# Weights requested behind the products that free their buffer, and small products of 48 keys in banks held for a stage

## The chip, the cores and the metric

The kernel runs on one core of a Trainium2 chip. The core has five engines with a queue each: TensorE (PE; its weight loads are shown apart, as PEld), VectorE (DVE), ScalarE (ACT), GpSimd (POOL) and SyncE (SP), which here issues all DMA transfers. The metric is the device time of one execution in microseconds, lower is better. Everything is in float32.

## The reference

The input x has 48 x 48 tokens of 768 channels. Layer 0 is a transformer block with 12 heads of 64 channels; layer 1 is a Fourier mixing layer, which the change doesn't touch. Cut to what matters here:

```
xn = layernorm(x, ln1_g, ln1_b)
q, k, v = split_heads(xn @ qkv_w + qkv_b)                # 12 heads, 2304 tokens, 64
attn = (q * scale) @ k.T                                   # 2304 x 2304 for each head
rel_h[h, w, kh] = q[h, w] . rel_pos_h[h - kh + 47]       # 48 numbers for each query
rel_w[h, w, kw] = q[h, w] . rel_pos_w[w - kw + 47]       # 48 numbers for each query
attn[(h, w), (kh, kw)] += rel_h[h, w, kh] + rel_w[h, w, kw]
out = softmax(attn) @ v
x = x + out @ proj_w + proj_b ; x = x + mlp(layernorm(x)) ; then layer 1
```

The "small products" of the title are `rel_h` and `rel_w`: for one row (or column) of queries, 48 queries against 48 rows of a table of 64 channels.

## The kernel before

Heads are worked on in six pairs, one head on partitions 0 to 63 and one on 64 to 127. The stage of projections lasts until about 453 us of the profile, the attention until about 1525 us, and then come the output projection, the MLP and layer 1.

**Projections** (`queries_keys_values`). Three passes p = 0, 1, 2 take 768 tokens each. At the start of a pass, `channels_first` transposes two groups of normalised rows into `xt`, and `sums_of_tokens` adds parts of them. Nine blocks follow: six calls of `queries_and_keys`, one for each head pair, and three of `values`. The order is written by hand in `orders`: in pass 0 the pairs come first, in pass 1 the values come first, and in pass 2 it is pair 0, the three values, and pairs 1 to 5. Each block forms a 2 x 2 product in seven products instead of eight (`seven`), of three matmul instructions each, and each instruction is recorded as two matmuls. The seven products rotate over four banks, `m0` to `m3`; evictions are L395 and L426 on ACT and L397, L399 and L428 on DVE. The four results of a block go through output tiles `o` (pool `stage`, 7 buffers) and are stored by SP (L429 for queries and keys, L460 for values).

The weights of a pair lie in one of two buffers, `pairs[slot]`. `weights_of` issues two DMAs of 384 KB each on SP (L348) and then four additions on POOL (`left`, L152 to L155), which form the sums that the seven products need; the value weights are fetched by `weights_of_values` (L334, two DMAs) and have additions of the same kind, three times as long. Where weights are asked for is written in the loop:

```
now = ahead
if pairs_left:
    ahead = weights_of(pairs_left.pop(0), slot % 2)
    slot += 1
queries_and_keys(p, i, *now)
```

Behind a block other work may be attached: `arrive` fetches three row tiles of x (L364 on SP) and normalises them (`normalise`, L116 to L124, mostly on DVE), after blocks 1 and 2 of the passes 0 and 1; `weights_of_values` after blocks 3 and 4 of pass 0; `constants` after block 5 of it; in pass 2, `fetch`, `columns` (twice after each of blocks 1 to 3), `relative` (after blocks 4, 6 and 8) and `fetch_values` (after block 5), which prepare pair 0 for the attention.

**Small products.** `columns(pr, i)` makes `rel_w` for 8 columns of queries, and `relative(pr, c)` makes `rel_h` for 8 rows. Each is 8 x 2 matmul instructions (L251, tile `wp`; L273, tile `hp`): one for each head of the pair, on array columns 0 to 63 and 64 to 127, with 48 queries moving and 64 rows of the table `relT` as weights, of which the kernel later uses 48. The queries of `columns` lie 16 elements apart in SBUF, those of `relative` in runs of 16. `two_parts` then splits the bank in a high and a low part (L222, L223 on ACT, L224 on DVE). `relative` also issues 24 DMAs on SP (L286, L290) that spread these parts into the tile `terms`.

The bank of a small product is a new tile for each call:

```
def small_bank(name):
    return banks["small"].tile([P, G], F32, name=name, tag="small")
```

In the stage of projections its pool has two buffers, in the attention one, which it shares with `den`, the sums of the softmax (L555).

**Attention.** For a pair and a group of 384 queries, `scores` (L525, L531, L535) runs over 18 tiles of 128 keys, in two runs of nine; `products` (L540) multiply the exponentials of the run before by v; `columns` and `relative` of what comes next, and `finish` of the last group, stand between the parts of `products`.

The order on PE and SP is that of the program (`manual_schedule`). The order on DVE, ACT and POOL is worked out by a scheduler when the program is built, so an edit on SP can move instructions there.

Of the kernel before, what the change touches and what calls it, by code (L numbers as in the profile page):

```python
# [9 lines left out]
F32 = mybir.dt.float32  # L10
# [5 lines left out]
PSUM = bass.MemoryType.PSUM  # L16
DRAM = bass.MemoryType.DRAM

P = 128
HW = 48  # L20
# [9 lines left out]
G = 384  # L30
# [14 lines left out]
def block_then_afno(  # L45
# [25 lines left out]
    nc = tc.nc  # L71
# [113 lines left out]
    with ExitStack() as flag_scope:  # L185
# [11 lines left out]
        with ExitStack() as att:  # L197
# [4 lines left out]
            relT = cst.tile([P, 2, 2, 112], F32, name="relT")  # L202
# [2 lines left out]
            r_pool = att.enter_context(tc.tile_pool(name="att_r", bufs=2))  # L205
            b_pool = att.enter_context(tc.tile_pool(name="att_b", bufs=3))

            banks = {}

            def small_bank(name):  # L210
                return banks["small"].tile([P, G], F32, name=name, tag="small")

            copies = [0]

# [29 lines left out]
            def columns(pr, i):  # L244

                qT = heads[pr][0].rearrange("p (c b h w) -> p b w c h", c=6, b=3, h=8)
                ps = small_bank("wp").rearrange("p (w c h) -> p w c h", w=8, h=8)
                for r in range(8):
                    w = 8 * i + r
                    for j in range(2):  # L250
                        nc.tensor.matmul(  # L251
                            ps[ts(j, 64), r], relT[:, j, 1, 47 - w : 111 - w],
                            qT[:, w // 16, w % 16], start=True, stop=True,
                        )
                hi, lo = (
                    a.rearrange("p (c b h w) -> p b w c h", c=6, b=3, h=8)[
                        :, i // 2, ds(8 * (i % 2), 8)
                    ]
                    for a in (col_hi, col_lo)
                )  # L260
                two_parts(hi, lo, ps)
# [3 lines left out]
            def relative(pr, c):  # L265

                qT = heads[pr][0][:, ts(c, G)].rearrange("p (b h w) -> p h b w", b=3, h=8)
                hp = small_bank("hp")
                ps = hp.rearrange("p (b h w) -> p h b w", b=3, h=8)
                for r in range(8):  # L270
                    h = 8 * c + r
                    for j in range(2):
                        nc.tensor.matmul(  # L273
                            ps[ts(j, 64), r], relT[:, j, 0, 47 - h : 111 - h], qT[:, r],
                            start=True, stop=True,
                        )
                row_hi = r_pool.tile([P, G], F32R, name="row_hi")
                row_lo = r_pool.tile([P, G], F32R, name="row_lo")
                two_parts(row_hi, row_lo, hp)
                terms = b_pool.tile([P, 3, 3, G], F32R, name="terms")  # L280
                ready[pr, c] = terms
                for j in range(2):
                    for n, (row, column) in enumerate(((row_hi, col_hi), (row_lo, col_lo))):
                        for i in range(3):
                            rows = ds(64 * j + 16 * i, 16)
                            nc.sync.dma_start(  # L286
                                out=terms[ds(64 * j + 16 * n, 16), i].bitcast(F32),
                                in_=row[rows].bitcast(F32).unsqueeze(1).to_broadcast([16, 3, G]),
                            )
                            nc.sync.dma_start(  # L290
                                out=terms[ds(64 * j + 32 + 16 * n, 16), :, i].bitcast(F32),
                                in_=column[rows, ts(c, G)].bitcast(F32)
                                .unsqueeze(1).to_broadcast([16, 3, G]),
                            )
# [11 lines left out]
            def queries_keys_values(qkv):  # L306
# [18 lines left out]
                upool = qkv.enter_context(tc.tile_pool(name="qkv_u", bufs=2))  # L325
                ln1 = qkv.enter_context(tc.tile_pool(name="ln1", bufs=3))
                psum = qkv.enter_context(tc.tile_pool(name="ps_qkv", bufs=1, space=PSUM))
                banks["small"] = qkv.enter_context(tc.tile_pool(name="ps_q", bufs=2, space=PSUM))

                wv = wpool.tile([P, NC, C], F32, name="wv")  # L330
                wvs = wpool.tile([P, 3, 3, CH], F32, name="wvs")
# [13 lines left out]
                def weights_of(pr, slot):  # L345
                    w, ws = pairs[slot]
                    for i in range(2):
                        nc.sync.dma_start(  # L348
                            out=w[:, :, i],
                            in_=qkv_w[:, ds(i * C + pr * P, P)].rearrange("(c p) f -> p c f", p=P),  # L350
                        )
                    left(
                        nc.gpsimd, w[:, 0:3, 0], w[:, 3:6, 0], w[:, 0:3, 1], w[:, 3:6, 1],
                        [ws[:, i] for i in range(3)],
                    )
                    return w, ws
# [114 lines left out]
                    orders.append(work)  # L471

                pairs_left = [i for work in orders for kind, i in work if kind == 0]
                ahead = weights_of(pairs_left.pop(0), 0)
                slot = 1
                for p in range(T // TB):
                    for g in (2 * p, 2 * p + 1):
                        channels_first(g)
                    sums_of_tokens(xt, xs)
                    for n, (kind, i) in enumerate(orders[p]):  # L480
                        if kind:
                            values(p, i)
                        else:
                            now = ahead
                            if pairs_left:
                                ahead = weights_of(pairs_left.pop(0), slot % 2)
                                slot += 1
                            queries_and_keys(p, i, *now)

                        if p == 0 and n in (3, 4):  # L490
                            weights_of_values(n - 3)
                        elif (p, n) == (0, 5):
                            constants()
                        elif p < 2 and n in (1, 2):
                            arrive(2 * p + 1 + n)
                        if p == 2 and n == 0:
                            fetch(0)
                        elif p == 2 and n in (1, 2, 3):
                            for j in (0, 1):
                                columns(0, 2 * (n - 1) + j)  # L500
                        elif p == 2 and n in (4, 6, 8):
                            relative(0, n // 2 - 2)
                        elif p == 2 and n == 5:
                            fetch_values(0)

            with tc.manual_schedule(engines={mybir.EngineType.PE, mybir.EngineType.SP}):
# [1 line left out]
                    queries_keys_values(qkv)  # L508

                psum = att.enter_context(tc.tile_pool(name="ps_att", bufs=1, space=PSUM))  # L510
                banks["small"] = psum
                kv_b = att.enter_context(tc.tile_pool(name="att_kv_b", bufs=1))
                o_pool = att.enter_context(tc.tile_pool(name="att_o", bufs=2))
                kv = [None, kv_b]
# [35 lines left out]

                def finish(pr, c, acc, ot):

                    den = small_bank("den")
                    for j in range(2):
                        nc.tensor.matmul(  # L555
                            den[ts(j, 64)], ones[:, 0:64], acc[:, j, :], start=True, stop=True
                        )
                    at = pr * (T // G) + c
                    rden = o_pool.tile([P, G], F32, name="rden", bufs=1)
                    nc.scalar.activation(  # L560
                        rden, den, AF.Identity, accum_out=sums[:, at : at + 1]
                    )

                    nc.vector.scalar_tensor_tensor(
                        ot, rden, col(V_VB + pr), ot, ALU.mult, ALU.add
                    )
                    nc.vector.reciprocal(rden, rden)  # L567
                    o = o_pool.tile([P, G], F32, name="o")
                    nc.vector.tensor_tensor(by_rows(o), by_blocks(ot), by_blocks(rden), ALU.mult)
                    nc.gpsimd.tensor_tensor(inverse, inverse, rden, ALU.add)  # L570
                    nc.sync.dma_start(out=oT[ts(pr, P), ts(c, G)], in_=o)
# [5 lines left out]
                for n, (pr, c, u) in enumerate(runs):  # L577
# [9 lines left out]
                    for i in range(RUN):  # L587
                        kt = RUN * u + i
                        p = exps[:, (RUN * n + i) % 18]
# [4 lines left out]
                    small = []  # L594
                    if u and c < 3:
                        small.append(partial(relative, pr, c + 3))
                    if pr < NC - 1:
                        if (c, u) in ((3, 1), (4, 0), (4, 1)):
                            i = 2 * (2 * (c - 3) + u - 1)
# [55 lines left out]
        with tc.tile_pool(name="ps_flag", bufs=1, space=PSUM) as psum, tc.tile_pool(  # L655
            name="ps_early", bufs=2, space=PSUM
# [29 lines left out]
        with tc.If(safe < 1):  # L686
            with ExitStack() as att:
                xnT = main.rearrange("p (c t) -> p c t", c=NC)
                with tc.tile_pool(name="g_ln1", bufs=3) as ln1, tc.tile_pool(
                    name="g_ps_ln1", bufs=2, space=PSUM  # L690
# [8 lines left out]
                psum = att.enter_context(tc.tile_pool(name="ps_gen", bufs=2, space=PSUM))  # L699
# [6 lines left out]
                relT = cst.tile([HD, 2, 112], F32, name="g_relT")  # L706
# [8 lines left out]
                for pr in range(NC):  # L715
                    w3 = []
                    for n, name in enumerate(("g_wq", "g_wk", "g_wv")):
                        w = w_pool.tile([P, NC, P], F32, name=name)
# [36 lines left out]
                    for sg in range(T // SG):  # L755
# [20 lines left out]
                        for i in range(2):  # L776
                            hp = psum.tile([P, G], F32, name="g_hp", tag="m")
                            for r in range(8):
                                h = sg * 16 + i * 8 + r
# [13 lines left out]
                        for i in range(2):  # L793
                            wp = psum.tile([P, 24, 16], F32, name="g_wp", tag="m")
                            for r in range(24):
                                w = i * 24 + r
# [584 lines left out]
```

## Time and profile before

| | us |
|---|---|
| median of 3 runs (3062.34 to 3068.3) | 3062.45 |
| the profiled execution | 3062.51 |
| its span, from the first to the last instruction | 3060.7 |
| PE busy | 2963.6 |
| DVE busy | 1783.4 |
| ACT busy | 868.6 |
| POOL busy | 572.1 |
| POOL waiting for `in_qkv_w_dram` in L152 | 345.5 |
| PE matmuls of L417 (`queries_and_keys`), 756 records | 253.0 |
| `wp` (L251), 1152 records, busy | 56.1 |
| `hp` (L273), 1152 records, busy | 40.7 |

Busy time of an engine is the time in which at least one of its instructions ran; PE and PEld overlap. A row of the groups names line, engine, operation, what is written and read, shapes and count, then busy time and mean duration in ns of one, then the idle time of the engine just ahead of it and what ended that. In a timeline the first column is the start, the second the length in us of a merged stretch, and "x32" the number of instructions in it. Rows of matmuls give the active rows and columns of the array ("128*64") and the moving shape ("128x48").

### The profile page before, as it was taken

The numbers are of one execution on the slowest core, as the hardware profiler recorded it, in microseconds if no ns is written. First come the engines' busy times: TensorE is split into PE (matmuls) and PEld (weight loads), VectorE is DVE, ScalarE is ACT, GpSimd is POOL, SyncE is SP. The second block draws the span as 40 slices with busy tenths as digits, with TensorE's granted clock in tenths as the row PEclk, the third lists the DMA queues.
The fourth block names the chain that finished last, engine by engine and source line by source line (L and its number), as shares of the span: only waits on it lengthen the run. The fifth ranks groups of instructions, "written<-read, shape, count | busy, mean of one in ns | idle before, by whom it ended". The sixth has DMA issues, their size and how long they took to land. (4 is left out here: it accounts for less than half of the span.)

```text
span 3060.7 us, 40413 instructions
## 1 busy us (share of the span) xinstructions
PE 2963.6 (97%) x15495; PEld 1796.0 (59%) x15495; DVE 1783.4 (58%) x2579; ACT 868.6 (28%) x1346; POOL 572.1 (19%) x510
## 2 busy tenths in 40 slices
PE   7999989999999999999999999989999999989998
PEld 4555645655556565555555555545555555548885
DVE  4243217777777777777624766666666566653443
ACT  1011115655556565555400211121101111011110
POOL 2203010000000000000133422342233222311210
PEclk9999999999999999999999999999999999999999
DMA  4433256173452617344332111121112211132324
GB/s 120 132 98 109 96 138 123 28 133 62 81 119 45 136 30 134 66 73 81 110 112 68 52 62 52 53 73 61 53 52 62 74 54 60 52 91 58 87 72 150
DMA packets 204144, 253.37 MB, mean 83 GB/s; under 512 B 21698, under 2 KB 185762, under 8 KB 202406
## 3 DMA queue, kind: packets, MB, share of 16 engines
q1 hardware_dynamic: 203942, 250.69, 32.5%
q8 instruction: 125, 2.05, 0.3%
q14 instruction: 77, 0.63, 0.1%
HBM read 136.77 MB, written 50.14 MB: 61 GB/s over the span
## 5 line engine op out<-in xcount | busy, mean ns | idle before, releaser
L592 DVE TENSOR_TENSOR acc<-acc,main 128x768 f32<-128x768 f32 x576 | 551.8, 958 | 202.6 <-ACT main L535 146.1
L535 ACT ACTIVATE main<-sp 128x768 f32<-128x768 f32 x648 | 522.1, 811 | 155.9 <-PE sp L531 148.6
L531 PE MATMUL sp<-terms,select 64*128 64x384 f32 x1296 | 411.9, 629 | 0.0
L989 DVE TENSOR_TENSOR main<-o,main 128x384 f32<-128x384 f32 x540 | 298.9, 556 | 43.2 <-PE o L987 4.8
L927 PE MATMUL h<-shared,w 128*128 128x384 f32 x864 | 297.1, 487 | 0.8 <-issue 0.8
L417 PE MATMUL m<-main 128*128 128x384 f32 x756 | 253.0, 495 | 23.9 <-DMA main<-in_qkv_w_dram 13.7
L525 PE MATMUL sp<-shared 64*128 64x384 f32 x1296 | 266.4, 488 | 1.6 <-ACT row_hi L223 1.0
L525 PE MATMUL sp<-qT,kT 64*128 64x384 f32 x1296 | 266.4, 487 | 0.0
L570 POOL TENSOR_TENSOR inverse<-inverse,rden 128x384 f32<-128x384 f32 x36 | 46.3, 1286 | 1032.6 <-DVE rden L567 968.9
L927 PEld LDWEIGHTS h<-shared,w 128*128 128x128 f32 x864 | 164.6, 191 | 116.3 <-issue 2.6
L927 PE MATMUL h<-shared,w1s 128*128 128x384 f32 x648 | 226.7, 486 | 0.0
L540 PE MATMUL op<-main,shared 128*64 128x384 f32 x1296 | 221.3, 488 | 0.0
L417 PEld LDWEIGHTS m<-main 128*128 128x128 f32 x756 | 144.4, 193 | 130.1 <-issue 26.1
L540 PE MATMUL op<-main,v 128*64 128x384 f32 x1296 | 220.0, 488 | 0.0
L933 ACT ACTIVATE hT<-c,vec 128x384 f32<-128x384 f32 x108 | 66.4, 615 | 466.5 <-DVE c L939 466.4
L939 DVE TENSOR_TENSOR c<-h,u 128x384 f32<-128x384 f32 x108 | 60.1, 557 | 212.4 <-PE h L927 212.4
L987 PE MATMUL o<-w,hT 128*128 128x384 f32 x432 | 176.3, 490 | 2.9 <-DVE mv L118 1.5
L987 PE MATMUL o<-w2s,hs 128*128 128x384 f32 x432 | 177.2, 492 | 1.0 <-DVE hs L153 1.0
L531 PEld LDWEIGHTS sp<-terms,select 64*128 64x128 f32 x1296 | 125.1, 186 | 83.9
L927 PEld LDWEIGHTS h<-shared,w1s 128*128 128x128 f32 x648 | 123.1, 190 | 85.9
L540 PEld LDWEIGHTS op<-main,v 128*64 128x64 f32 x1296 | 90.6, 138 | 106.4 <-issue 106.4
L525 PEld LDWEIGHTS sp<-shared 64*128 64x128 f32 x1296 | 116.9, 186 | 59.7 <-issue 20.3
(157 smaller groups left out, 3888.7 us busy)
## 6 DMA issues: line engine op xcount, KB each, us to landing
w<-in_mlp_w_dram SPq DMA_DIRECT2D x72, 768.0 KB
terms<-col_parts SPq DMA_DIRECT2D x432, 72.0 KB
terms<-row_hi SPq DMA_DIRECT2D x216, 72.0 KB
terms<-row_lo SPq DMA_DIRECT2D x216, 72.0 KB
main<-in_qkv_w_dram SPq DMA_DIRECT2D x36, 384.0 KB
z<-zt SPq DMA_DIRECT2D x48, 150.0 KB
z<-y SPq DMA_DIRECT2D x50, 144.0 KB
zo<-z SPq DMA_DIRECT2D x12, 600.0 KB
```

Source lines behind the costliest of these rows:

```text
L417: nc.tensor.matmul(bank, a[:, c, :], b[:, c, :], start=(first and c == 0), stop=(c == 2), skip_group_check=not first,)
L525: nc.tensor.matmul(sp[:, j, :G], kT[at, ts(kt, P)], qT[at, ts(c, G)], start=True, stop=False,)
L531: nc.tensor.matmul(sp[:, j, :G], select[at, a % 2], ready[pr, c][at, a // 2, b], start=False, stop=True,)
L535: nc.scalar.activation(p, sp[:, :, :G], AF.Exp, scale=HD**-0.5)
L540: nc.tensor.matmul(op[ts(j, 64)], v[:, kt0 + i, ts(j, 64)], ps[i][:, j, :], start=(kt0 + i == 0), stop=(kt0 + i == NT - 1),)
L570: nc.gpsimd.tensor_tensor(inverse, inverse, rden, ALU.add)
L592: nc.vector.tensor_tensor(acc, made[0] if kt == 1 else acc, p, ALU.add)
L927: nc.tensor.matmul(bank[i], a[:, c, :], b[:, c, :], start=(start and c == 0), stop=(c == 2), skip_group_check=not start,)
L933: nc.scalar.activation(h[:, i, ts(k, G)], src, AF.Gelu, bias=col(V_B1 + 2 * n + i))
L939: nc.vector.tensor_tensor(t, src, other, ALU.add)
L987: nc.tensor.matmul(bank[k], a, b, start=start, stop=True, skip_group_check=not start)
L989: nc.vector.tensor_tensor(dst, bank[k], dst, ALU.add)
```

## The change

In the loop over blocks, the weights of the first two pairs are asked for ahead of the loop; then each block of a pair is issued first, and behind it the weights for the pair after the next, into the buffer that the block has just read. In `columns` and `relative` the weights are 48 rows of the table instead of 64, and the products write 48 partitions of each half. The banks of the small products are tiles made once for a stage, two in the projections and one in the attention (shared with `den` as before), set to zero by DVE when they are made and handed out in turn.

```diff
-            banks = {}
-
-            def small_bank(name):
-                return banks["small"].tile([P, G], F32, name=name, tag="small")
+            banks = []
+
+            def small_banks(psum, n):
+
+                banks[:] = [psum.tile([P, G], F32, name=f"small{i}") for i in range(n)]
+                for bank in banks:
+                    nc.vector.memset(bank, 0.0)
+
+            def small_bank():
+                banks.append(banks.pop(0))
+                return banks[-1]
...
-                ps = small_bank("wp").rearrange("p (w c h) -> p w c h", w=8, h=8)
+                ps = small_bank().rearrange("p (w c h) -> p w c h", w=8, h=8)
...
-                            ps[ts(j, 64), r], relT[:, j, 1, 47 - w : 111 - w],
+                            ps[ds(64 * j, HW), r], relT[:, j, 1, 47 - w : 95 - w],
...
-                            ps[ts(j, 64), r], relT[:, j, 0, 47 - h : 111 - h], qT[:, r],
+                            ps[ds(64 * j, HW), r], relT[:, j, 0, 47 - h : 95 - h], qT[:, r],
...
-                banks["small"] = qkv.enter_context(tc.tile_pool(name="ps_q", bufs=2, space=PSUM))
+                small_banks(qkv.enter_context(tc.tile_pool(name="ps_q", bufs=1, space=PSUM)), 2)
...
-                ahead = weights_of(pairs_left.pop(0), 0)
-                slot = 1
+                ahead = [weights_of(pairs_left.pop(0), i) for i in range(2)]
+                slot = 0
...
-                            now = ahead
+                            queries_and_keys(p, i, *ahead.pop(0))
                             if pairs_left:
-                                ahead = weights_of(pairs_left.pop(0), slot % 2)
+                                ahead.append(weights_of(pairs_left.pop(0), slot % 2))
                                 slot += 1
-                            queries_and_keys(p, i, *now)
...
-                banks["small"] = psum
+                small_banks(psum, 1)
```

More of the change, by code (lines that the diff above doesn't have):

```diff
@@ L267, in relative @@
                 qT = heads[pr][0][:, ts(c, G)].rearrange("p (b h w) -> p h b w", b=3, h=8)
-                hp = small_bank("hp")
+                hp = small_bank()
                 ps = hp.rearrange("p (b h w) -> p h b w", b=3, h=8)
@@ L551, in finish @@
                 def finish(pr, c, acc, ot):
-                    den = small_bank("den")
+                    den = small_bank()
                     for j in range(2):
```

## The prediction

> **What bounds the kernel now.** I read the page first: TensorE is busy for 97% of the span, so time comes only from making its work shorter or from the few places where it stands still. The waits of TensorE, asked for the stage of projections alone (0 to 453 us), name them; then the windows of that stage, block by block, show their size. A block is one `queries_and_keys` or `values` call: 21 products, each recorded as two matmuls. An undisturbed block takes 13.54 us from its start to the next one's, 13.74 where a small product follows.
>
> ```profile
> PE 2963.6 (97%) x15495; PEld 1796.0 (59%) x15495; DVE 1783.4 (58%) x2579; ACT 868.6 (28%) x1346; POOL 572.1 (19%) x510
> ...
> L417 PE MATMUL m<-main 128*128 128x384 f32 x756 | 253.0, 495 | 23.9 <-DMA main<-in_qkv_w_dram 13.7
> ```
>
> Columns of the windows: length, TensorE busy (matmuls), granted clock, share of the DMA engines, GB/s.
>
> ```profile
> 377.95:391.69 13.74, 13.74 (x46) 1.00 0.62 108
> 391.69:398.48 6.79, 0.07 (x1) 0.72 0.78 170
> 398.48:413.71 15.23, 15.23 (x42) 0.90 0.77 223
> 414.78:428.52 13.74, 13.74 (x46) 1.00 0.62 108
> 428.52:435.53 7.01, 0.08 (x2) 0.77 0.79 166
> 435.53:451.01 15.48, 15.48 (x43) 0.88 0.26 93
> ```
>
> The reader should see two holes of 7 us, both put down to the weights' DMA, and after each a block that is slow because the clock was withdrawn. The timeline of SP's queue says why the weights are late:
>
> ```profile
> 377.63 0.32 SPq L429 DMA_DIRECT2D q_d<-o  x1
> 378.95 0.75 SPq L286 DMA_DIRECT2D terms<-row_hi  x1
> ...
> 393.85 0.59 SPq L290 DMA_DIRECT2D terms<-col_parts  x1
> 394.56 1.14 SPq L348 DMA_DIRECT2D main<-in_qkv_w_dram  x2
> ```
>
> The 24 copies of `relative` fill SP from 378.95 to 394.44, and the weights are asked for only then, 3 us after the next block wanted to start (377.95 + 13.54 = 391.49).
>
> The small products themselves (timeline of TensorE), and the rows that price a weight load by its columns (groups by form):
>
> ```profile
> 376.88 1.14 PE L273 MATMUL hp<-shared,relT 128*64 128x48 f32 x32
> ```
> ```profile
> 554.26 1.60 PE L251 MATMUL wp<-qT,relT 128*64 128x48 f32 x32
> ```
> ```profile
> 2858.62 0.33 PE L1155 MATMUL lp<-xf,shared 96*96 96x48 f32 x2
> 2858.80 0.33 PE L1156 MATMUL lp<-xf,shared 96*96 96x48 f32 x2
> 2858.97 0.46 PE L1137 MATMUL fp<-shared,zi 96*96 96x96 f32 x3
> ```
>
> Matmuls go in pairs, one for each half of the array. Taking off the last one's own 222 ns (263 for `wp`), a pair of `hp` comes every (1.14 - 0.222) / 15.5 = 59 ns, one of `wp` every 86 ns. The `lp` rows with 48 moving columns start 0.17 to 0.18 us apart for two: 85 to 90 ns each although only 48 columns stream, so their 96 weight columns set the pace.
>
> [...] `wp` streams queries 64 bytes apart, `hp` runs of 16 neighbours, and only `wp` takes 86 ns. [...]
>
> **The change, part by part.** The sum is against the profiled execution, 3062.51 us (3060.7 of span), which is the median (3062.45) for this purpose.
>
> *Weights asked for behind the products.* Before, the load for block n+1 is issued at the start of block n; after, the load for n+2 at the end of block n. Both come when the same buffer falls free, so no load gains a block of lead. What changes is what stands ahead of it on SP: the normalised rows' loads (L364), the value weights (L334), the constants, the copies of `relative` and `fetch_values` now stand behind the two weight DMAs. Those wait for TensorE's last product of the block, but the four stores before them have already waited for its eviction, so the added wait is 0; behind it, all of the above start some 1.2 us later (the issue time of two).
>
> - The third pass (p = 2). Holes: 398.48 - 391.49 = 6.99 and 435.53 - 428.32 = 7.21. Cold blocks: 15.23 and 15.48 against 13.74, 1.49 and 1.74. All go: asked for at about 378 and landing 5 us later, weights are wanted at 405. **-17.4 us.** What is late next: the copies, by 1.2 us; the `terms` they fill are read first at 453. The stores of the next block wait behind the copies until some 395, as before; seven output tiles cover the four of one block and three of the next (third eviction near 403).
> - The second pass. The block 207.31 to 225.56 takes 18.25, since DVE takes row statistics while the weights share the DMA: rows asked for at 208.50 arrive until 220.65. The block before, with the same rows' work but no weights on the way, takes 15.18. The load disappears from there (it now goes out before the pass), so 18.25 becomes about 15.3: **-2.9.**
> - The first pass, blocks of 16.27 and 17.23. Rows now follow the weights. Weights alone arrive in 4.4 us (issued 45.28 to 46.4, POOL starts at 50.35). They then stop slowing the rows, so the third row tile lands when it did, within 1 us: 0 (-2 to +5). The built order also puts L399 ahead of the statistics, which ends the first half of the stall; the eviction L428 still stands behind them and ends the second, so no gain is taken.
> - POOL: `left` of a pair (4 x 1.0) now stands ahead of `left` of the value weights (4 x 2.6, from 111.85). The values' block begins at 118.15 and needs the second sum 2 us later: from about 114.5 it is ready at 119.7, the third at 122.3 against 122.0: **+0.5** (0 to 2).
>
> *Order at the border.* In the changed program the last eviction (L428) stands behind `row_lo` (L224) on DVE, and the first `sp` waits for it. Before, `sp` starts at 453.11, freed by ACT. After: `row_lo` from 453.09, 0.56, then the eviction 0.62: **+1.1.**
>
> *48 keys.* Same 1152 small instructions. `hp`: weights fall from 64 to 48 columns, [...] 36 blocks x 15.5 pairs x 14 ns = **-7.9 us.** In the attention stage TensorE is busy 170.00 of 170 us from 530 to 700, so this counts in full. `wp`: [...] the stream binds and 64 columns hide under it: 0 (-8 to 0).
>
> *Held banks.* Two memsets of 128x384 on DVE at the start (0.38 each, as `inverse`), under its 5.21 us of waiting for the first rows; one at the border, under the 3.5 us in which DVE waits for the first exponentials. If that cover went, 0.4 each. The products lose a wait of TensorE for itself; no idle time stands before `den` on TensorE, so 0 (to -3.7: 72 x 51 ns, the queue's shortest wait).
>
> Sum: -17.4 - 2.9 + 0.5 + 1.1 - 7.9 = -26.6; 3062.5 - 26.6 = **3035.9 us**.
>
> **Rivals.**
> - *The columns are not what paces `hp`* (a floor on issue, or the bank's writes, in runs of 16). For it: two matmuls in 59 ns is already quick. Against it: `lp` follows its weights. Only the loads gain: 3043.8. Chance 0.10.
> - *`wp` follows its weights too*, if load and stream compete; its loads are longer (153 ns against 138). Then about 8 more: 3028. Chance 0.10.
> - *The first pass pays for the third*: rows wait a full weight load, 3.7 us in each of two blocks, +7.4: 3043. For it: DVE stands in those very rows now. Chance 0.10.
> - *The holes only move*: the stores behind the copies run out of tiles, or the copies slow the weights, and half of the 17.4 returns: 3044.6. Against it: weights have 27 us and seven tiles do. Chance 0.06.
> - *Slower*: a tile of 48 columns no longer shares the array, and the two halves go one after the other. Place: all 1116 pairs (15.5 x 72). Price: [...] +61 against -18.7 of the rest: 3105. It decides from 18.7 us / 1116 = 17 ns a pair. Against it: the built program keeps tiles of 128x64 at columns 0 and 64, and a 48-column load in the trace (`mp`, 122 ns) is in line with 138 at 64. Chance 0.05.
>
> **How the numbers follow.** The forecast has 0.59 and gives 3036. What a measurement of this kernel can tell from no change is some 0.2%, 6 us. All cases but the last are faster by more; 0.02 is for the case that gains are eaten to within 6 us. Range: 3025 (with `wp`) to 3047 (rivals at 3044, and 3 for the first pass); outside lie the slower case and sums of two rivals.
>
> **What would show it.** Right: no wait of TensorE for `in_qkv_w_dram`; SP's weight issues directly behind the block's last store; all p = 2 blocks near 13.6; `hp` blocks of about 0.92 us [...], `wp` blocks still 1.6; attention beginning at about 434; a wait of 2 us before the first `sp`. Wrong: `hp` still 1.14; more than 5 us lost in either of the two slow blocks of the first pass; a `wp` block near 3 us.

## The result, and the profile after

The changed kernel takes 3039.3 us (median of 5, 3038.2 to 3044.5) against 3062.3 (median of 5, 3058.9 to 3068.3): a ratio of 0.9936, 95% interval 0.9919 to 0.9952, or 23 us less. The forecast was 3036.0. The profiled execution took 3041.24 us with a span of 3039.4. Its page, first the engines, then the row that answers to L417:

```profile
PE 2947.5 (97%) x15495; PEld 1783.8 (59%) x15495; DVE 1784.6 (59%) x2582; ACT 869.5 (29%) x1346; POOL 569.2 (19%) x510
...
L424 PE MATMUL m<-main 128*128 128x384 f32 x756 | 250.1, 492 | 13.5 <-DVE o L435 8.9
```

TensorE is busy 16.1 us less with the same number of instructions. The wait in front of the products of queries and keys has another name: 13.7 us of it were put down to the weights' DMA, now 8.9 are put down to `o` of L435, DVE's eviction. So the holes of the third pass are gone, and something else has begun. The windows of the third pass, block by block (length, TensorE busy with its matmuls, weight loads, DVE, ACT, POOL, granted clock, DMA share, GB/s):

```profile
387.59:401.24 13.65, 13.65 (x46) 8.09 (x43) 2.91 (x5) 1.92 (x4) 3.91 (x4) 1.00 0.90 156
401.24:414.88 13.64, 13.64 (x44) 7.79 (x42) 2.97 (x5) 1.06 (x2) 1.00 (x1) 1.00 0.88 210
415.74:429.38 13.64, 13.64 (x46) 8.08 (x43) 3.44 (x6) 1.92 (x4) 5.68 (x7) 1.00 0.88 190
429.38:443.02 13.64, 13.64 (x43) 7.79 (x41) 2.97 (x5) 1.06 (x2) 0.64 (x1) 1.00 0.75 173
```

No hole is left, and the clock is full behind them: 54.57 us for four blocks that took 71.99 before, **-17.4**. SP's timeline shows why:

```profile
387.49 0.32 SPq L436 DMA_DIRECT2D q_d<-o  x1
387.91 1.07 SPq L355 DMA_DIRECT2D main<-in_qkv_w_dram  x2
389.08 0.75 SPq L293 DMA_DIRECT2D terms<-row_hi  x1
...
405.39 0.59 SPq L297 DMA_DIRECT2D terms<-col_parts  x1
```

The two weight DMAs now stand between the last store of the block and the copies, 13.3 us ahead of the block that reads them (401.24). The small products, on TensorE's timeline:

```profile
596.60 0.93 PE L280 MATMUL small<-qT,relT 128*48 128x48 f32 x32
```
```profile
563.48 1.58 PE L258 MATMUL small<-qT,relT 128*48 128x48 f32 x32
```

`hp` fell from 1.14 to 0.93 us, `wp` from 1.60 to 1.58. The attention stage, from the first `sp` to the first `pp`, went from 1071.2 to 1063.5 us.

What has begun is in the waits of TensorE (us in total, times, longest):

```profile
PE m L424 <- DVE o L435: 8.9, 3, 4.2
...
PE sp L531 <- DVE o L435: 2.2, 1, 2.2
PE m L455 <- POOL wvs L153: 1.5, 1, 1.5
```

and in the windows of the first pass: the third, fourth and fifth blocks of pairs, and the first block of values. Before, they took 16.27, 17.23, 13.54 and 13.54.

```profile
60.99:80.43 19.44, 15.29 (x43) 8.69 (x42) 8.28 (x20) 1.83 (x5) 3.91 (x4) 0.91 0.44 147
80.43:98.98 18.55, 14.75 (x43) 8.34 (x42) 8.27 (x20) 1.83 (x5) 3.90 (x4) 0.95 0.45 148
98.98:113.25 14.27, 14.27 (x44) 8.37 (x42) 2.97 (x5) 1.06 (x2) 3.90 (x4) 0.95 0.58 188
126.79:142.72 15.93, 14.08 (x43) 7.82 (x42) 4.69 (x7) 0.96 (x2) 12.54 (x8) 1.00 0.38 116
```

Two engines' timelines name the cause. First SP, then DVE, in the block that starts at 60.99:

```profile
62.26 1.07 SPq L355 DMA_DIRECT2D main<-in_qkv_w_dram  x2
63.38 1.92 SPq L371 DMA_DIRECT2D x<-in_x_dram  x3
```
```profile
70.78 1.02 DVE L116 BATCH_NORM_STATS2 stats<-x 128x6 f32<-128x384 f32 x2 [3.22 <-DMA x<-in_x_dram]
...
76.21 1.09 DVE L435 SCALAR_TENSOR_TENSOR o<-m,vec,u 128x384 f32<-128x384 f32 x2
```

The rows are asked for at 63.38, behind the weights; the first of them is on DVE only at 70.78, 7.4 us later. DVE's order is fixed, with the statistics of all three row tiles ahead of the eviction L435. While DVE stands before data that has not come (3.22 us of idle time in front of the first row), the accumulators that TensorE needs are not emptied.

The two profiled executions, cut at the first `sp` and the first `pp`, differ by -7.0 us ahead of the attention, -7.7 in it and -6.6 behind it. The last of these is in no step of the prediction, and that code is the same in both kernels. The account of the prediction below takes it up.

### The profile page after: what moved, and what is told of

It reads as the page before. It is cut to its first block, busy times and chain, and to the rows that moved or that the text cites. A ratio compares the mean times of both kernels' runs of the same rounds, so it can differ in the third digit from the quotient of the medians.

```text
span 3039.4 us, 40414 instructions
## 1 busy us (share of the span) xinstructions
PE 2947.5 (97%) x15495; PEld 1783.8 (59%) x15495; DVE 1784.6 (59%) x2582; ACT 869.5 (29%) x1346; POOL 569.2 (19%) x510
## 5 line engine op out<-in xcount | busy, mean ns | idle before, releaser
L424 PEld LDWEIGHTS m<-main 128*128 128x128 f32 x756 | 144.3, 192 | 117.0 <-issue 16.1
```

Source lines behind the costliest of these rows:

```text
L424: nc.tensor.matmul(bank, a[:, c, :], b[:, c, :], start=(first and c == 0), stop=(c == 2), skip_group_check=not first,)
```

## The experiments

Theory: the gain is the third pass (-17.4) and the columns of `hp` (-8), and three costs are paid back: rows behind weights in the first pass, the order on POOL, the order on DVE at the border. Rivals: the held banks give part of it; the distance at which weights are asked for gives it, not what stands ahead of them; `wp` too is paced by its weights.

**The two halves, and the banks.** `loads_only` is the kernel before with the new loop over blocks; `keys_only` is the changed kernel with this put back:

```diff
-                ahead = [weights_of(pairs_left.pop(0), i) for i in range(2)]
-                slot = 0
+                ahead = weights_of(pairs_left.pop(0), 0)
+                slot = 1
...
-                            queries_and_keys(p, i, *ahead.pop(0))
+                            now = ahead
                             if pairs_left:
-                                ahead.append(weights_of(pairs_left.pop(0), slot % 2))
+                                ahead = weights_of(pairs_left.pop(0), slot % 2)
                                 slot += 1
+                            queries_and_keys(p, i, *now)
```

`keys64` is the changed kernel with 64 columns: `ps[ds(64 * j, 64), r], relT[:, j, 0, 47 - h : 111 - h]`, and the same in `columns`.

> The kernel before with the new order of the weights alone: 64 keys and the banks from the pool stay. If the keys bring only the shorter weight loads of hp (36 blocks x 0.22 us = 7.9), this kernel takes 3039.3 + 7.9 = 3047 us, and its stages behind the attention start as late against its own attention's start as in the changed kernel. If the 6.6 us that the changed kernel gains behind the attention stage (which no step of the prediction has) belong to the keys or the held banks, it takes 3047 + 6.6 = 3054. hp blocks 1.07 to 1.14 us in both; no hole in the third pass; first pass as slow as in the changed kernel (19.4 and 18.6 us for its third and fourth block of pairs).

> The changed kernel with the weights asked for as before: 48 keys and held banks alone. By the theory 3062.3 - 7.9 = 3054.4 us, with both holes of 7 us in the third pass, the first pass as before (16.3 and 17.2 us), the first sp released by ACT, and hp blocks of 0.93 us or less. If the keys or the held banks also gave the 6.6 us of the late stages: 3048. If small products of 48 columns are no faster in this order either: 3062.

> The changed kernel with 64 columns of weights in both small products, in the held banks. If the banks cost and bring nothing, the attention stage takes 1071.2 us as before (1063.5 in the changed kernel) and hp blocks 1.07 to 1.14. If part of the 7.7 us came from the banks, it takes less than 1071.2 by that part.

Measured: `loads_only` 3047.35 us, ratio 0.9949 (0.9932 to 0.9967); `keys_only` 3053.81, ratio 0.9971 (0.9960 to 0.9982), both against 3061.73 before. The gains of 14.4 and 7.9 add up to 22.3, the whole within its uncertainty. The attention stage took 1071.2 us in `loads_only`, 1063.6 in `keys_only`, and 1072.0 in the one run of `keys64`: held banks with 64 columns bring nothing, the columns bring all of it. The slow blocks of the first pass in `loads_only` took 17.96 and 18.33 us, less than the 19.4 and 18.6 expected. The part of the expectations on the late stages failed: by its profile neither half has the 6.6 us (1536.2 and 1539.6 us from the first `pp` to the end, 1536.4 before, 1529.8 in the changed kernel).

**What stands ahead of the weights.** `copies_first` moves one call within the third pass:

```diff
                             queries_and_keys(p, i, *ahead.pop(0))
+                            if p == 2 and n in (4, 6, 8):
+                                relative(0, n // 2 - 2)
                             if pairs_left:
                                 ahead.append(weights_of(pairs_left.pop(0), slot % 2))
                                 slot += 1
...
-                        elif p == 2 and n in (4, 6, 8):
-                            relative(0, n // 2 - 2)
```

> The changed kernel with one thing undone in the third pass alone: the copies of relative are asked for ahead of the weights again, behind the same products. DVE's last eviction comes ahead of row_lo at the border again, too. By the theory both holes return with their slow blocks, +17.4, and the border gives 1.2 back: 3039.3 + 16.2 = 3055.5 us, third pass with blocks near 20.5, 15.2, 20.7, 15.5. Rival (the distance at which the weights are asked for is what helps, since the load now belongs to the block after the next): holes of under 2 us, 3040.

Measured: 3055.55 us, ratio 0.9982 (0.9973 to 0.9990). The waits of TensorE and the first two windows of the third pass in its profile:

```profile
PE m L424 <- DMA main<-in_qkv_w_dram: 13.3, 2, 6.7
```
```profile
378.65:399.03 20.38, 14.08 (x58) 8.11 (x52) 3.67 (x7) 1.92 (x4) 0.00 (x0) 0.92 0.67 124
399.03:414.35 15.32, 15.05 (x42) 8.69 (x42) 2.35 (x4) 1.06 (x2) 7.79 (x8) 0.89 0.75 222
```

The hole, the slow block behind it and 16.2 us of the gain come and go with the copies alone. The rival of the distance falls: the buffer comes free at the same moment in both orders, and the block that reads it is the same.

**Rows, value weights, border.** `rows_first` asks for the rows ahead of the weights in the first pass. `best` also asks for the value weights first, and has POOL make `row_lo` in the third pass; `best2` lets POOL do so only at the border:

```diff
                             queries_and_keys(p, i, *ahead.pop(0))
+                            if p == 0 and n in (1, 2):
+                                arrive(1 + n)
+                            if p == 0 and n in (3, 4):
+                                weights_of_values(n - 3)
                             if pairs_left:
...
-                            relative(0, n // 2 - 2)
+                            relative(0, n // 2 - 2, nc.gpsimd if n == 8 else nc.vector)
```

> The changed kernel with the rows of x asked for ahead of the weights in the first pass (two places), otherwise the same. If the first pass is slow because the rows wait until the weights are through, its third and fourth blocks go back from 19.4 and 18.6 to 16.3 and 17.2 us and the clock behind them recovers: -5.2, 3034.1 us. Rival (DVE's order is the cause, the statistics stand ahead of the evictions whichever comes first): 3039. Second rival: the weights then come too late and the next block of pairs waits for them: slower than 3039, with a wait for in_qkv_w_dram.

> The changed kernel with its three costs taken away: in the first pass the rows and the value weights are asked for ahead of the pairs' weights, and in the third pass row_lo is made by POOL, so that the last eviction has nothing ahead of it on DVE. By the theory -4 (rows), -2 (value weights' sums, the first values' block back at 13.54) and -1.2 (border): 3039.3 - 7.2 = 3032 us. If these costs only show up elsewhere (POOL's row_lo is twice as long and late for the first terms; the pairs' weights come too late behind the value weights): 3039 or more, with a wait for them by name.

> As best, but POOL makes row_lo only for the last of the three row terms, at the border: in best, the second one stood on POOL ahead of the sums of a pair's weights and waited 19 us for its source, and the products waited 1.9 us for the sum (block of 15.84). By the theory that block goes back to 13.65 and nothing else changes: 3033.5 - 2.2 = 3031 us. If the block was slow for another reason (the copies share the DMA with the weights), it stays near 15.8 and 3033.

Measured: `rows_first` 3040.03 us, ratio 0.9929 (0.9915 to 0.9943): its median shows no gain over the changed kernel, against the expectation. Its blocks do: 16.79, 17.55 and 13.54, in sum 47.9 where the changed kernel's first profile has 52.3. On DVE, in the block that starts at 57.93:

```profile
64.33 1.02 DVE L116 BATCH_NORM_STATS2 stats<-x 128x6 f32<-128x384 f32 x2 [1.71 <-DMA x<-in_x_dram]
...
72.00 0.56 DVE L435 SCALAR_TENSOR_TENSOR o<-m,vec,u 128x384 f32<-128x384 f32 x1
```

Asked for at 59.15, the first row is on DVE after 5.2 us instead of 7.4, and the eviction comes 14.1 us into the block instead of 15.2. The spread of single executions, some 10 us, hides a difference of 4 in medians of six; over all profiles it stands out. In seven with rows behind the weights the three blocks took 50.0 to 53.5 us, mean 51.4; in six with rows ahead 47.0 to 47.9, mean 47.4. **The new order costs 4.0 us there**, much of it as a withdrawn clock: (1 - granted clock) x length of these blocks is 3.4 us in the mean of the seven and 0.6 in that of the six. Likewise the first values' block: 14.87 to 15.93 (mean 15.24) in eight profiles with the value weights behind a pair's, 13.54 in all six with them ahead: **1.7 us.**

`best` took 3033.48 us, ratio 0.9916 (0.9900 to 0.9932), 1.5 above what was expected, and its waits have a new one. POOL's timeline:

```profile
PE m L424 <- POOL main L153: 1.9, 1, 1.9
```
```profile
404.12 1.00 POOL L231 TENSOR_TENSOR row_lo<-shared,row_hi 128x384 fp32r<-128x384 f32 x1 [19.02 <-ACT row_hi L230]
405.07 0.99 POOL L152 TENSOR_TENSOR main<-main 128x384 f32<-128x384 f32 x1
```

`row_lo` (1.00 us on POOL, 0.56 on DVE) stood ahead of the sums of a pair whose weights were long there, and waited for its source. The block behind took 15.84 us. In `best2` it takes 13.65 again, and the first `sp` waits 1.0 us for ACT as before the change. `best2` took 3027.54 us, ratio 0.9888 (0.9872 to 0.9905), 3.5 under the expectation, which its blocks do not explain.

**Rows much earlier.** `early` is `best2` with `arrive` split into the asking and the normalising; the normalising stays where it was:

```diff
                 ahead = [weights_of(pairs_left.pop(0), i) for i in range(2)]
                 slot = 0
+                ask(2)
...
                     sums_of_tokens(xt, xs)
+                    if p == 0:
+                        ask(3)
```

> As best2, but the rows of the second pass are asked for much earlier: the third group right behind the first weights, the fourth ahead of the first block; DVE's statistics then stand in the first block and a little ahead of it. If what is left of the first pass's loss (3.8 and 2.8 us over 13.54 in best) is rows that arrive slowly beside weights and stores, blocks three and four become 13.54, and the first block pays once for the fourth group: +2 to +6 in place of 6.7, so 3027 to 3031 us. If the statistics themselves (some 6 us of DVE for each group) are what holds the evictions, or the early rows delay the first weights, the first blocks lose 7 us or more and the time is 3031 to 3038.

Measured: 3025.5 us, ratio 0.9886 (0.9868 to 0.9904), the quickest of the kernels that keep the results, and below the 3027 to 3031 expected. Its windows for the three blocks of pairs shown above of the changed kernel:

```profile
59.09:72.63 13.54, 13.54 (x43) 7.98 (x42) 2.97 (x5) 1.06 (x2) 3.90 (x4) 1.00 0.36 116
72.63:86.18 13.55, 13.55 (x44) 7.98 (x43) 2.97 (x5) 1.06 (x2) 3.90 (x4) 1.00 0.36 116
86.18:99.72 13.54, 13.54 (x44) 7.98 (x42) 2.97 (x5) 1.06 (x2) 3.36 (x4) 1.00 0.64 205
```

The planner put the statistics of both groups, some 10 us of DVE, into the first block of pairs and the start of the second (31.55 to 48.6 us), and these two blocks still took 15.12 and 13.54 us, no more than in the other kernels. The first transposes took 15.84, within the 14.3 to 17.4 of the others. So the same statistics need not hold TensorE once their rows are there. Two things changed together, though: the rows came early, and the planner set evictions among the statistics (at 39.94, 43.84 and 46.04 us) where the changed kernel has them behind. No run separates the two. That `early` beats `best2` is seen in these blocks (40.6 against 47.7 us), not in the medians, whose intervals overlap.

**What paces the small products.** `wp_runs` lets `columns` stream 48 neighbouring queries; `keys32` gives both products 32 columns:

```diff
-                            qT[:, w // 16, w % 16], start=True, stop=True,
+                            heads[pr][0][:, ds(48 * (w // 2), 48)], start=True, stop=True,
```
```diff
-                            ps[ds(64 * j, HW), r], relT[:, j, 0, 47 - h : 95 - h], qT[:, r],
+                            ps[ds(64 * j, 32), r], relT[:, j, 0, 47 - h : 79 - h], qT[:, r],
```

> The changed kernel with the products of columns reading 48 neighbouring queries in place of queries 64 bytes apart (the values of rel_w are then those of other queries; instructions, shapes and weights are the same). If the strided stream is what paces wp, a pair of products comes as quickly as in hp, 47 ns: a block falls from 1.58 to 15.5 x 0.047 + 0.26 = 0.99 or to 0.93 us, 36 blocks, -21 to -23 us in all, some 3017 us. If its weight loads or the bank pace it, the block stays 1.5 to 1.6 and the time 3039.

> The changed kernel with 32 columns of weights in both small products (a third of the keys is left out, and the scale of the exponential is 1e-6 to keep the numbers finite; nothing else is changed). If the weight loads still pace hp at 48 columns, a pair falls [...] from 46.6 to 33: a block of 15.5 x 0.033 + 0.21 = 0.72 us. If the 48 streamed columns pace it from here on, the block stays near 0.9. wp, if its stream paces it, stays at 1.5 to 1.6 us either way.

Measured, TensorE's timeline of `wp_runs` and of `keys32`:

```profile
537.07 0.93 PE L258 MATMUL small<-qT,relT 128*48 128x48 f32 x32
```
```profile
591.05 0.88 PE L280 MATMUL small<-qT,relT 128*32 128x48 f32 x32
```

With neighbouring queries a `wp` block takes what an `hp` block takes, 0.93 us; the attention stage falls to 1045.5 us, and the one run of the kernel to 3014.6. The stride of the stream is what separates the two: a pair of `wp` takes 82.8 ns with queries 64 bytes apart and 45.0 with neighbours. With 32 columns `hp` hardly falls further: the starts of its matmuls in the attention stage lie 29.3 ns apart at 64 columns, 22.9 at 48 and 21.6 at 32, or 58.6, 45.8 and 43.2 ns a pair. The step from 64 to 48 columns saves 12.8 ns, the next 16 only 2.6: below 48 something else sets the pace. It may be the 48 streamed columns: a block's 42 matmuls of 384 columns take 13.54 us, 0.84 ns a column, which gives an estimate of 40 ns for 48. A least distance between matmuls, the prediction's first rival, would look the same, and no run changed the number of streamed columns. The time of `keys32`, 3049.2 us in one run, went up by 10; the last section has what its trace shows of it.

**Both kernels once more.**

> The changed kernel once more, on the chip of the other runs of this call. The third pass, the border, hp and wp must repeat to 0.1 us (they follow from an order). The first pass's third to fifth blocks of pairs (52.3 us in its first profile, 50.1 and 51.3 in two other kernels with rows behind the weights, 47.0 to 47.9 with rows ahead) should lie between 50 and 52.5. If the 6.6 us of the late stages and the 3.5 us of the start are spread between executions, they come out different here; if they belong to the change, they repeat. Median 3039.

> The kernel before once more, for a second profile of it. What follows from an order must repeat: third pass 20.5, 15.2, 20.7, 15.5 us, first pass near 47.0 for its third to fifth blocks, hp 1.07 to 1.14, attention stage 1071.2 us. If the stages behind the attention differ between executions and not between the kernels, their 1536.4 us need not repeat: the changed kernels showed 1527 to 1540 in code that is the same. If they follow the order of the weights' loads, they come out at 1535 or more again.

Measured: the changed kernel 3038.1 us, ratio 0.9930 (0.9915 to 0.9944), profiled span 3030.6; the kernel before 3065.24 (one run), span 3063.4. What follows from an order repeats: third pass 54.6 and 72.0 us, attention 1063.5 and 1071.2. Others do not: the first transposes took 17.40 us in the changed kernel's first profile and 14.32 in this one, the first pass's three blocks 52.3 and 50.0. The first `sp` comes at 446.1 and at 435.9 us. The late stages took 1538.0 us in the second profile of before, 1531.2 in that of after.

## Why the prediction was right, and where it was off

The time lies in the range and the direction is as forecast. The terms, with what the profiles measured in their place:

| step | predicted | measured |
|---|---|---|
| third pass, holes and cold blocks | -17.4 | -17.4 |
| second pass (end of values, first pair) | -2.9 | -2.5 (mean of 11 against 3 profiles, each spread over 3 us) |
| first pass, rows behind weights | 0 (-2 to +5) | +4.0 |
| POOL, sums of the value weights | +0.5 (0 to 2) | +1.7 |
| border, eviction behind `row_lo` | +1.1 | +1.2 (wait 2.2 against 0.96) |
| 48 keys | -7.9 | -8.4 (attention -7.7, projections -0.7) |
| held banks | 0 | 0 |
| sum | -26.6 | -21.4 |

The medians say -23.

- **Third pass: right, with one wrong number.** The text says that weights asked for at about 378 are wanted at 405 and have 27 us. They are wanted one block later, at 391.5 by the same rows; in the changed kernel 13.3 us lie between. This was enough, since the load, beside the copies, takes 6.3 us there and POOL's sums 4.0 (from 387.91 to 394.25, and to 398.24), but it is half of what was claimed, and `copies_first` shows it used up by 16 us of copies.
- **First pass: the term that was mis-sized.** The step "Rows now follow the weights. Weights alone arrive in 4.4 us ... They then stop slowing the rows" looked at when the third tile lands and not at who stands waiting for the first. The rows are asked for 1.2 us later in the block (2.39 us after its start against 1.22 in `rows_first` and in the kernel before) and reach DVE 2.2 us later after the ask (7.4 us against 5.2); the evictions behind them are late too, and part of the delay returns as a withdrawn clock (0.91 and 0.95). This is the third rival, at about half the 7.4 us that it was priced at: it is no rival, it happens beside the main theory. `early` shows the step that was not taken: the stall was there before the change, and all of it could be taken away.
- **POOL: right mechanism, too small.** The value weights' sums were taken to start near 114.5 and be ready at 119.7, ahead of a block that would itself be later. POOL's timeline of the changed kernel:

```profile
121.06 1.00 POOL L152 TENSOR_TENSOR main<-main 128x384 f32<-128x384 f32 x1 [11.64 <-DMA main<-in_qkv_w_dram]
...
125.00 2.62 POOL L152 TENSOR_TENSOR wvs<-wv 128x1152 f32<-128x1152 f32 x1
127.71 2.61 POOL L153 TENSOR_TENSOR wvs<-wvs,wv 128x1152 f32<-128x1152 f32 x1
```

  The pair's sums wait for their own weights until 121.06, so those of the values start at 125.00, 1.8 us ahead of the block of values (126.79), where the estimate had 3.6 (114.5 against 118.15). The second sum is there at 130.3, 3.5 us into the block.
- **48 keys: right in size, and the weights set the pace as said down to 48.** The 14 ns a pair were the author's estimate, from 59 at 64 columns to 45 at 48; the rows of the trace before, 85 at 96 columns (`lp`) and 59 at 64 (`hp`), give an estimate of 46 on a straight line. Measured: 45.8. That `wp` would stay was right as well (84.2 ns a pair before, 82.8 after), and `wp_runs` shows that its stream is the cause: 45.0 with neighbouring queries.
- **Right by its own signs, and one against it:** no wait for `in_qkv_w_dram`, `hp` 0.93 where 0.92 was named, a wait of 2.2 us at the border. The sign named for "wrong", more than 5 us lost in one of the two slow blocks, came too (19.44 - 13.54 = 5.9). The attention's start, forecast for about 434, came at 446.1 in the first profile and at 435.9 in the second.
- **In no step: the 6.6 us behind the attention, which are mostly the clock of these two executions.** From the first `pp` to the end, the fourteen profiles fall into two groups, seven at 1527.1 to 1531.5 us and seven at 1535.4 to 1539.6, though the code there is the same in all. `best` and `best2`, which differ in who makes two of the row terms, lie on different sides, and `loads_only` and `keys64`, with the new order of loads, are in the upper group, so the order of the loads alone does not set it. The granted clock does part the groups: (1 - clock) x time over this stretch is 20.5 to 27.3 us in the lower group and 29.5 to 33.4 in the upper (25.7 in the changed kernel, 30.8 before), and without it all fourteen take 1502.6 to 1507.9. One such place in the MLP, before and then changed; in both, TensorE has waited 1.50 us ahead of the same product:

```profile
1698.62:1702.03 3.41, 1.76 (x5) 0.59 (x4) 3.41 (x9) 1.41 (x2) 3.41 (x3) 1.00 0.00 0
1702.03:1705.45 3.42, 3.42 (x7) 1.61 (x6) 2.51 (x6) 0.17 (x1) 0.11 (x1) 0.50 0.02 5
```
```profile
1680.81:1684.22 3.41, 1.87 (x6) 0.53 (x4) 3.41 (x10) 0.90 (x2) 3.41 (x3) 1.00 0.00 0
1684.22:1687.64 3.42, 3.24 (x9) 1.73 (x10) 3.00 (x8) 0.68 (x1) 0.63 (x1) 1.00 0.00 0
```

  The stretch behind the wait runs at half the clock in one kernel and at the full clock in the other. Over all executions with a clock on record, 52 of the kernel before and ten of the changed one, the mean times differ by 22.4 us and the mean losses to the clock by 3.0 (36.1 against 33.1); the two profiled executions differ by 9.4 in it (39.8 against 30.4). So a good part of the 6.6 us is the luck of this pair. How much of the 23 us is owed to the late stages in a typical pair stays open; the terms above give 21.4 without them.
- **The clock, behind shorter waits too.** The prediction counts a withdrawn clock behind the holes of 7 us alone. In the first of the windows above TensorE stood for 1.65 us of 3.41, and the stretch behind had a granted clock of 0.50; in the third it stood for 1.54, and the stretch behind had 1.00.

## What to carry to other kernels

When a request moves within a queue, price what it is moved past as well as what it is moved for: here one queue gave 17.4 us in the third pass and took 4.0 and 1.7 in the first, by the same rule. Work that is ready can stand behind work that waits for data: DVE sat idle for 3.22 us in front of the first row, with the eviction L435 behind it. Here, asking earlier for that data was worth more than reordering the requests (three blocks in 40.6 us, against 47.4 reordered and 51.4). Before narrowing weights, find what else streams beside them: at 48 columns `hp` was within 3 ns a pair of what it takes at 32 (45.8 against 43.2), and `wp`, whose stream is strided, gained 1.4 from 64 to 48 (84.2 against 82.8).

## What the runs showed of the hardware

- In `keys32`, tiles of 32 columns among tiles of 64 cost more than they saved: the attention stage took 1073.7 us in one run against 1063.5 (some 0.8 of it may be a withdrawn clock, as in the 1064.3 of `rows_first`). From a small product's last matmul to the next product with `v` it takes 136 ns (`hp`) and 191 (`wp`) instead of 38 and 78; from a product with `v` into a small one 416 instead of 316 to 318. That is some 0.1 us more at each change between the two widths; the trace does not show the cause. With 48 columns there is no such step: 38 and 78 ns against 52 and 76 before.
- Statistics of some 10 us on DVE, spread over little more than one block with evictions among them, cost TensorE nothing in `early`, where their data was there (the two blocks took 15.12 and 13.54 us, no more than elsewhere), while half of them in front of late rows cost it 2.6 to 6.5 us a block in the other thirteen profiles.
- In the traces of the kernel before and of the changed one the granted clock is full or half (1.00 or 0.50), and the halved stretches within a trace start whole multiples of 3.41 us apart. Each of these 25 stretches follows 3.41 us of this grid in which TensorE stood for at least 1.65 us, but in the kernel before 1.77 us of standing in 84.11 to 87.52 were not followed by one. By an estimate from these stretches a short wait can cost a further 1.7 us (half of 3.41) or nothing: the wait of 1.50 us in the MLP came ahead of a halved stretch before and of a full one in the changed kernel.
